# A two-layer graph network on one core: the end of each round put in another order

## The chip, the core and the metric

The kernel runs on one core of a Trainium2 chip. Such a core has five engines that work side by side: TensorE (PE) for matrix products and transposes, VectorE (DVE), ScalarE (ACT), GpSimd (POOL) and SyncE (SP). Each works through its own queue in the order in which the program was built. Here SP only issues transfers (DMAs). Matrix products land in PSUM, everything else lives in SBUF. The metric is the device time of one execution in microseconds (us), lower is better.

## The reference, cut to what matters

There are 64 graphs of 256 nodes with 512 features, each with its own 256 x 256 adjacency matrix. Two layers follow each other, both with a residual and a layer norm ahead of them.

```
h = relu(layernorm(x))                       # layer 0: gated attention, 8 heads of 64
q, k, v = h Wq', h Wk', h Wv'
attn = softmax(q k' / 8, masked by adj)      # per head
c = attn v
gate = sigmoid([c, h] Wg' + bg)
x = x + gate * h + (1 - gate) * c
h = relu(layernorm(x))                       # layer 1: one attention head with additive scores
Wh = h W
e = leaky_relu(Wh a1 + (Wh a2)'), masked by adj
x = x + elu(softmax(e) Wh)
```

All is float32.

## The kernel before

The kernel is a software pipeline over graphs. `emit_round(i)` (L480 to L544) writes one round, and the rounds run from -1 to 65. In a round, four graphs are in four stages: p = i + 1 gets its q, k, v and the first half of its scores, graph i gets its softmax and its weighted values c, q = i - 1 its gate, residual and Wh, and r = i - 2 its last attention and output. A graph's attention is done in two halves of four heads. Half 0 of the scores of graph p is computed at the end of the round before the one in which the rest of that graph's attention is done.

The steps of this case:

- `a_scores(g, half)` (L296): 16 matmul records on PE into four PSUM tiles of the pool "w", which has five buffers. It also takes the SBUF tile `e` for the exponentials.
- `a_softmax(g, half, jj)` (L314): for two heads, four passes on DVE that scale, mask and write `e` (L322), four exponentials on ACT (L326), a reciprocal on DVE (L330), and four multiplications on POOL (L333).
- `a_transpose(g, half)` (L337): four transposes of 32 x 32 blocks on DVE from `e` to `eb` (L344), and then 16 DMAs on SP from `eb` to `eT` (L349).
- `a_weigh(g, half)` (L352): 16 matmul records of v with `eT` (L362, tile `pc`), and a copy on ACT to `cT` (L135). In the second half it also forms the sums `S_c` on POOL (`token_sums`, L140 to L150): four operations, which the gate's products need.
- `g_gate`, `g_wh`, `p_qk`, `p_v`: products by Strassen's scheme (`strassen`, L152): seven block products in three parts, with three PSUM tiles ma, mb, mc that only these products use. Part 0 has products 1, 6 and 5, part 1 has 7 and 2, part 2 has 4 and 3. DVE and ACT combine them (L172, L176, L186). Product 6 of the gate is the first to read `S_c`, and it reads the second of the four sums (L147, `S_c<-S_c,cT`), which is made from the first one (L146).
- `g_diff` (L388): `d`, the difference of h and c, in two halves on POOL (L393).

Three things set the order. PE and SP run in the order in which `emit_round` writes them (`tc.manual_schedule`, L546). The order on DVE, ACT and POOL is chosen by the framework's scheduler when the program is built, so it can change where only the order of the calls changes. Buffers add waits of their own. The pool "e" has two buffers, and `e`, `eb` and `eT` all come from it in turn:

```
        "x": 5, "adj": 1, "mask": 4, "hT": 3, "S": 3, "qk": 3, "v": 2, "wh": 1, "e": 2,
```

So the tile `e` of the next graph's half 0 takes the buffer that held `eb` of the present graph's half 1. It cannot be written until the 16 DMAs that read that `eb` have landed. These are the DMAs that `a_weigh(i, 1)` waits for.

Of the kernel before, what the change touches and what calls it, by code (L numbers as in the profile page):

```python
# [22 lines left out]
def kernel(  # L23
# [78 lines left out]
    def weight_sums(key):  # L102

        w = weight[key]
        t = const.tile([P, 3, 2, w.shape[3]], F32, name=f"w{key}_t")
        b11, b12, b21, b22 = (w[:, r:r + 2, n, :] for r in (0, 2) for n in range(2))
        nc.vector.tensor_tensor(t[:, 1], b22, b12, ALU.subtract)
        nc.vector.tensor_tensor(t[:, 0], t[:, 1], b11, ALU.add)
        nc.vector.tensor_tensor(b12, b12, b11, ALU.subtract)
        nc.vector.tensor_tensor(t[:, 2], b21, t[:, 0], ALU.subtract)  # L110
        weight[key] = {1: b11, 2: b21, 3: b22, 4: t[:, 2], 5: b12, 6: t[:, 0], 7: t[:, 1]}
# [10 lines left out]
    def edge_columns():  # L122

        w = weight["1"]
        for c in range(HC):
            for side in range(2):
                scr = sb["tmp"].tile([P, 2, HH], F32, tag="t", name=f"scr_{c}_{side}")
                nc.vector.scalar_tensor_tensor(
                    scr, w[:, c, :, :HH], 1.0, a_sb[side].rearrange("p (n f) -> p n f", n=2),
                    ALU.mult, ALU.mult, accum_out=w[:, c, side, HH:],  # L130
                )
# [348 lines left out]
    def emit_round(i):  # L480


        parts = {}

        def step(fn, g, *args):
            if 0 <= g < B:
                fn(g, *args)

        def part(fn, g, n):
            if 0 <= g < B:  # L490
                if n == 0:
                    parts[fn] = fn(g)
                parts[fn][n]()

        p, q, r = i + 1, i - 1, i - 2
        step(load_graph, p + 1)
        part(g_gate, q, 0)
        step(a_softmax, i, 0, 1)
        step(g_diff, q)
        step(g_edges, r)  # L500
        part(g_gate, q, 1)
        step(p_sums, p)
        step(a_transpose, i, 0)
        part(g_gate, q, 2)
        step(g_mix, q)
        step(g_transpose, r)
        if i == -1:
            weight_sums("q")
            weight_sums("k")
        part(p_qk, p, 0)  # L510
        step(g_residual, q)
        step(g_out, r, 0)
        step(a_scores, i, 1)
        step(g_norm, q)
        step(a_softmax, i, 1, 0)
        part(p_qk, p, 1)
        step(a_weigh, i, 0)
        step(a_softmax, i, 1, 1)
        part(p_qk, p, 2)
        step(g_transpose_h, q)  # L520
        step(a_transpose, i, 1)
        if i == -1:
            weight_sums("v")
        part(p_v, p, 0)
        step(g_out, r, 1)
        if i == 0:
            weight_sums("gh")
            weight_sums("gc")
            nc.vector.tensor_scalar_mul(hbg, hbg, 0.5)
        part(p_v, p, 1)  # L530
        step(p_stats, p + 1)
        part(p_v, p, 2)
        if i == 0:
            edge_columns()
            weight_sums("1")
        part(g_wh, q, 0)
        step(p_norm, p + 1)
        step(p_transpose, p + 1)
        step(g_sums, i)
        step(a_weigh, i, 1)  # L540
        part(g_wh, q, 1)
        step(a_scores, p, 0)
        step(a_softmax, p, 0, 0)
        part(g_wh, q, 2)  # L544

    with tc.manual_schedule(engines={mybir.EngineType.PE, mybir.EngineType.SP}):  # L546
        load_graph(0)
        load_weight("q", nc.sync)
        load_weight("k", nc.scalar)
        load_weight("v", nc.sync)  # L550
        p_stats(0)
        p_norm(0)
        p_transpose(0)
        for i in range(-1, B + 2):
            if i == 0:
                load_weight("gh", nc.sync)
                load_weight("gc", nc.sync)
                load_weight("1", nc.sync)
                load_small()
            emit_round(i)  # L560
            graphs.pop(i - 2, None)
# [32 lines left out]
```

## Time and profile before

| | |
|---|---|
| three runs | 3481.12, 3485.15, 3485.97 us; median 3485.15 |
| profiled execution | span 3484.6 us, 68023 instructions, granted TensorE clock 0.991 |
| PE busy | 3324.3 us, 95% |
| DVE, POOL, ACT busy | 2294.7 us (66%), 1637.9 us (47%), 1338.4 us (38%) |
| DMA | 262.50 MB, mean 75 GB/s |

Busy time counts an engine's instructions alone. Matmuls are pipelined and their ends are modelled, so that the recorded end of one reaches a little past the start of the next. The waits of an engine are attributed to what came last, by semaphores. A round takes about 53 us. With PE at 95% what matters is what stands in the remaining time of PE: every wait of PE adds to the whole, while waits of the other engines cost nothing as long as PE has its next product in time.

### The profile page before, as it was taken

To read this page: it belongs to the slowest core of one execution; us is meant where nothing else is said; L and a number is where in the kernel's file an instruction comes from. 1 tells how busy PE (TensorE), PEld (TensorE's weight loads), DVE (VectorE), ACT (ScalarE), POOL (GpSimd) and SP (SyncE) were. 2 spreads that over 40 slices of the span, in tenths; PEclk is the share of its full clock that TensorE was granted. 3 is DMA by queue.
4 is the path that set the end of the run, shared out by engine and by line. 5 is a ranking of instruction groups with operands and counts; after the bars stand their busy time and mean duration, and the time that the engine had idled before them with its cause. 6 is when DMAs were issued, how large, how long until landed. Compare 5 with 4: busy or idle time off the path is not lost.

```text
span 3484.6 us, 68023 instructions
## 1 busy us (share of the span) xinstructions
PE 3324.3 (95%) x23944; PEld 2865.9 (82%) x23944; DVE 2294.7 (66%) x6184; ACT 1338.4 (38%) x3778; POOL 1637.9 (47%) x2439
## 2 busy tenths in 40 slices
PE   6999999999999999999999999999999999999996
PEld 5888888888888888888888888888888888888874
DVE  6666667667667667667666666676676676666653
ACT  2334334343344334334334343443433443333432
POOL 2454454454454454544544544544544545435433
PEclk9999999999999999999999999999999999999998
DMA  4232332322322322322323323323323223223221
GB/s 138 66 85 68 77 80 66 83 71 73 87 69 71 89 68 70 90 68 72 87 70 72 84 66 80 79 66 84 73 70 87 69 70 90 68 70 82 64 59 31
DMA packets 432195, 262.50 MB, mean 75 GB/s; under 512 B 310768, under 2 KB 333296, under 8 KB 431856
## 3 DMA queue, kind: packets, MB, share of 16 engines
q1 hardware_dynamic: 430800, 257.11, 30.0%
q8 instruction: 191, 3.13, 0.4%
q14 instruction: 148, 1.21, 0.1%
q10 hardware_dynamic: 1056, 1.05, 0.1%
HBM read 57.15 MB, written 33.55 MB: 26 GB/s over the span
## 4 chain that ended last, share of the span: by engine, by line
PE 59%; SPq 16%; DVE 12%; POOL 4%; DMA 4%; issue 3%; ACT 1%; DVEq 0%; POOLq 0%; ACTq 0%
SPq L349 16%; PE pmb_z L162 10%; PE pma_z L162 6%; PE pmc_z L162 6%; PE pmb_qk L162 6%; PE pc L362 5%; PE ps L306 5%; PE pma_qk L162 5%; PE pmc_qk L162 4%; PE pmb_wh L162 4%; DMA eT<-eb 4%; DVE e L322 2%; POOL e L333 2%; DVE bs_l L201 2%; PE pma_wh L162 2%
## 5 line engine op out<-in xcount | busy, mean ns | idle before, releaser
L333 POOL TENSOR_SCALAR e<-e,rec 128x256 f32<-128x256 f32 x1024 | 473.7, 482 | 256.0 <-DVE rec L330 133.5
L206 POOL TENSOR_TENSOR rs_l<-ve_l,mhalf 128x2 f32<-128x2 f32 x128 | 90.6, 708 | 1021.2 <-DVE ve_l L204 1017.3
L326 ACT ACTIVATE e<-e,low 128x256 f32<-128x256 f32 x1024 | 506.1, 496 | 84.3 <-DVE low L322 59.0
L322 DVE CUSTOM_DVE_ANT_0 e<-ps,mask 128x256 f32<-128x256 f32 x1024 | 375.1, 418 | 74.9 <-PE ps L306 71.6
L344 DVE STREAM_TRANSPOSE eb<-e 128x512 f32<-128x512 f32 x512 | 345.6, 694 | 88.4 <-POOL e L333 88.3
L362 PE MATMUL pc<-eT,v 128*64 128x256 f32 x2048 | 259.0, 396 | 111.7 <-DMA eT<-eb 103.0
L172 DVE TENSOR_TENSOR u_wh<-pmb_wh,u_wh 128x257 f32<-128x257 f32 x128 | 54.7, 427 | 408.7 <-PE pmb_wh L162 408.7
L472 ACT ACTIVATE pos<-po,rec 128x512 f32<-128x512 f32 x128 | 88.0, 687 | 604.6 <-DVE mv_l L202 415.3
L362 PEld LDWEIGHTS pc<-eT,v 128*64 128x64 f32 x2048 | 150.9, 140 | 193.4 <-issue 115.2
L306 PEld LDWEIGHTS ps<-qk 64*128 64x128 f32 x2048 | 187.3, 186 | 86.0 <-issue 68.8
L306 PE MATMUL ps<-qk 64*128 64x256 f32 x2048 | 255.7, 389 | 0.0
L465 PE MATMUL po<-wh,egT 128*128 128x512 f32 x512 | 245.8, 603 | 0.8 <-DVE egT L137 0.8
L444 ACT ACTIVATE eg<-eg,nm 128x256 f32<-128x256 f32 x128 | 64.0, 501 | 384.1 <-DVE nm L441 384.1
L475 POOL TENSOR_TENSOR x<-x,pos 128x512 f32<-128x512 f32 x128 | 163.0, 1274 | 98.0 <-DVE pos L474 98.0
L215 ACT ACTIVATE h_l<-x,nb_l,rs_l 128x512 f32<-128x512 f32 x256 | 201.8, 813 | 14.5 <-DVE nb_l L212 7.3
L135 ACT COPY cT<-pc 128x512 f32<-128x512 f32 x128 | 73.8, 577 | 327.6 <-PE pc L362 327.6
L326 ACT ACTIVATION_READ_ACCUMULATOR e<-e,low 128x1 f32 x1024 | 192.3, 188 | 0.0
L402 ACT ACTIVATE z<-z,hbg 128x256 f32<-128x256 f32 x256 | 116.2, 501 | 186.6 <-DVE z L172 186.6
L148 POOL TENSOR_TENSOR S_l<-hT_l 128x256 f32<-128x256 f32 x128 | 93.7, 732 | 166.5 <-DVE hT_l L137 166.5
L201 DVE BATCH_NORM_STATS2 bs_l<-x 128x6 f32<-128x512 f32 x256 | 167.8, 677 | 5.0 <-DMA x<-in_x_dram 5.0
L146 POOL TENSOR_TENSOR S_c<-cT 128x256 f32<-128x256 f32 x64 | 46.4, 725 | 255.2 <-ACT cT L135 255.2
L393 POOL TENSOR_TENSOR d<-hT_l,cT 128x512 f32<-128x512 f32 x128 | 162.5, 1270 | 0.0
(142 smaller groups left out, 8359.1 us busy)
## 6 DMA issues: line engine op xcount, KB each, us to landing
eT<-eb SPq DMA_DIRECT2D x2048, 64.0 KB, 2.0
x<-in_x_dram SPq DMA_DIRECT2D x64, 512.0 KB, 4.1
out_dram<-x SPq DMA_DIRECT2D x64, 512.0 KB, 2.9
hT_l<-h_l SPq DMA_DIRECT2D x1008, 32.0 KB, 2.0
adj<-in_adj_dram SPq DMA_DIRECT2D x64, 256.0 KB, 4.2
wk_sb<-in_L_gnn_Wk_dram ACTq DMA_DIRECT2D x2, 512.0 KB, 6.9
wq_sb<-in_L_gnn_Wq_dram SPq DMA_DIRECT2D x2, 512.0 KB, 8.7
wv_sb<-in_L_gnn_Wv_dram SPq DMA_DIRECT2D x2, 512.0 KB, 10.4
```

What stands on the lines that cost most here:

```text
L162: nc.tensor.matmul(bank[key][(slice(None), *cols)], lhsT, rhs, start=first and i == 0, stop=last and i == len(todo) - 1, skip_group_check= ...
L201: nc.vector.bn_stats(bs, xt[:, t, :])
L215: nc.scalar.activation(h[:, t, :], xt[:, t, :], AF.Relu, bias=nb[:, t:t + 1], scale=rs[:, t:t + 1])
L306: nc.tensor.matmul(psc[jj, i][:, t, :], qk[r:r + DK, 0, jj, t * P:(t + 1) * P], qk[r:r + DK, 1, jj, :], start=True, stop=True,)
L322: nc.vector.tensor_tensor_reduce(es[:, i, t, :], psc[jj, i][:, t, :], mask[:, t, :], -SCALE, HUGE, ALU.add, ALU.min, accum_out=low[:, i, t ...
L326: nc.scalar.activation(es[:, i, t, :], es[:, i, t, :], AF.Exp, bias=low[:, i, t:t + 1], scale=-1.0, accum_out=sums[:, i, t:t + 1],)
L333: nc.gpsimd.tensor_scalar(es[:, i, t, :], es[:, i, t, :], rec[:, i, t:t + 1], 1.0, ALU.mult, ALU.mult)
L344: nc.vector.transpose(blocks[:, :, 4 * h:4 * h + 4, :].rearrange("p b n c -> p n b c"), e[:, h])
L349: nc.sync.dma_start(eT[32 * j:32 * j + 32, i], blocks[32 * i:32 * i + 32, j])
L362: nc.tensor.matmul(pc[i * DK:(i + 1) * DK, jj, :].rearrange("p (t a c) -> p t a c", t=NT, c=32), s["v"][:, kc, hd * DK:(hd + 1) * DK], eT[ ...
L465: nc.tensor.matmul(pm, s["egT"][:, kc, t * P:(t + 1) * P], s["wh"][:, kc, :, :HH], start=(kc == 0), stop=(kc == NT - 1))
L475: nc.gpsimd.tensor_tensor(s["x"][:, t, :], s["x"][:, t, :], pos, ALU.add)
```

## The change

The calls at the end of the round are put in another order. Before, after part 0 of Wh, PE had: the weighted values of half 1 of graph i, Wh part 1, the scores of half 0 of graph p, Wh part 2. After it: the scores, Wh part 1, the weighted values, Wh part 2. The softmax that follows the scores (first two heads, `a_softmax(p, 0, 0)`) moves with them.

```
@@ -537,10 +537,10 @@
         step(p_norm, p + 1)
         step(p_transpose, p + 1)
         step(g_sums, i)
-        step(a_weigh, i, 1)
-        part(g_wh, q, 1)
         step(a_scores, p, 0)
         step(a_softmax, p, 0, 0)
+        part(g_wh, q, 1)
+        step(a_weigh, i, 1)
         part(g_wh, q, 2)
 
     with tc.manual_schedule(engines={mybir.EngineType.PE, mybir.EngineType.SP}):
```

The program holds the same instructions as before, in the same number on each engine. On PE two blocks change places. On SP nothing moves: none of the three steps issues a DMA. On POOL, as the program is built, a round of the middle now runs: one sum of `S_c` that needs only the first half of `cT` (L148), the four multiplications of the first two heads (L333), the four of the other two heads, then the first sum (L146), the second half of `d` (L393), the second sum (L147) and the fourth (L149). Before, these three sums and `d` stood ahead of the eight multiplications. On ACT the eight exponentials now stand ahead of the copy to `cT`, with the copy of Wh's product 2 (L186) between the seventh and the eighth. On DVE the eight passes now stand ahead of the additions of Wh part 1, but for the last pass, which follows the first of these additions.

More of the change, by code (lines that the diff above doesn't have):

```diff
@@ L539, in emit_round @@
         step(g_sums, i)
-        step(a_weigh, i, 1)
-        part(g_wh, q, 1)
         step(a_scores, p, 0)
         step(a_softmax, p, 0, 0)
+        part(g_wh, q, 1)
+        step(a_weigh, i, 1)
         part(g_wh, q, 2)
```

## The prediction

> **What bounds the kernel now.** I read the busy shares and the chain that ended last first.
>
> ```profile
> PE 3324.3 (95%) x23944; PEld 2865.9 (82%) x23944; DVE 2294.7 (66%) x6184; ACT 1338.4 (38%) x3778; POOL 1637.9 (47%) x2439
> PE 59%; SPq 16%; DVE 12%; POOL 4%; DMA 4%; issue 3%; ACT 1%; DVEq 0%; POOLq 0%; ACTq 0%
> ```
>
> PE is nearly full, yet 16% of the chain is SP's issuing: PE is overtaken by transfers somewhere. The second view was the waits of PE alone, from 130 to 3380 us, the 62 middle rounds (waited for; us, times, longest):
>
> ```profile
> PE pc L362 <- DMA eT<-eb: 86.5, 60, 2.6
> PE pc L362 <- issue: 3.7, 2, 2.1
> ```
>
> This is the whole answer: PE waits once a round, always ahead of `pc`, for 90.2 / 62 = 1.45 us on average. The timeline of PE over all rounds puts each of them at half 1; half 0 never waits. From one `pc` to the next a round takes 51.43 to 51.49 us plus its wait in nearly every round, so this wait decides the pace. The end of a round (start, us, instruction, idle before):
>
> ```profile
> 1719.99 1.03 PE L162 MATMUL pmc_wh<-w_sb,S_l 128*128 128x257 f32 x4
> 1722.11 1.95 PE L362 MATMUL pc<-eT,v 128*64 128x256 f32 x16 [1.09 <-DMA eT<-eb]
> 1723.98 1.14 PE L162 MATMUL pmb_wh<-w_t,S_l 128*128 128x257 f32 x4
> 1724.96 1.03 PE L162 MATMUL pma_wh<-w_sb,hT_l 128*128 128x257 f32 x4
> 1725.92 2.00 PE L306 MATMUL ps<-qk 64*128 64x256 f32 x16
> 1727.85 1.14 PE L162 MATMUL pmb_wh<-w_t,hT_l 128*128 128x257 f32 x4
> 1728.82 1.03 PE L162 MATMUL pmc_wh<-w_sb,S_l 128*128 128x257 f32 x4
> 1729.69 1.05 PE L162 MATMUL pma_z<-hT_l,wgh_sb 128*128 128x128 f32 x8
> 1730.58 1.06 PE L162 MATMUL pma_z<-cT,wgc_sb 128*128 128x128 f32 x8
> 1731.47 1.06 PE L162 MATMUL pmb_z<-S_g,wgh_t 128*128 128x128 f32 x8
> 1732.36 1.06 PE L162 MATMUL pmb_z<-S_c,wgc_t 128*128 128x128 f32 x8
> ```
>
> The reader is to see start-to-start spacings (ends overlap) and that `S_c` is needed last. The chain in time shows what releases `pc`: the last of 16 issues, each about 0.63 us, and its landing.
>
> ```profile
> 1720.00 1.98 DMA eT<-eb
> 1721.97 0.14 issue
> 1722.11 1.95 PE pc L362 x16
> ```
>
> Last, DVE and POOL in the same stretch:
>
> ```profile
> 1727.08 0.42 DVE L322 CUSTOM_DVE_ANT_0 e<-ps,mask 128x256 f32<-128x256 f32 x1 [1.03 <-PE ps L306]
> ...
> 1724.76 0.73 POOL L146 TENSOR_TENSOR S_c<-cT 128x256 f32<-128x256 f32 x1 [3.25 <-ACT cT L135]
> 1725.44 1.27 POOL L393 TENSOR_TENSOR d<-hT_l,cT 128x512 f32<-128x512 f32 x1
> 1726.67 0.73 POOL L147 TENSOR_TENSOR S_c<-S_c,cT 128x256 f32<-128x256 f32 x1
> ...
> 1729.93 1.85 POOL L333 TENSOR_SCALAR e<-e,rec 128x256 f32<-128x256 f32 x4 [1.73 <-DVE rec L330]
> 1732.10 1.85 POOL L333 TENSOR_SCALAR e<-e,rec 128x256 f32<-128x256 f32 x4 [0.32 <-DVE rec L330]
> ```
>
> Here the sums `S_c` are ready at 1727.4 and PE asks for them at 1732.36: 5 us to spare. The change spends this reserve.
>
> **What the Trainium skill says.** "Perfetto Trace Analysis", Per-instruction lifecycle: DVE, ACT and GpSimd run strictly first in, first out, and TensorE's ends are estimates. The trace agrees: `pmc_wh` ends at 1721.02 by the record while its successor, unhindered, would start at about 1720.95. "SBUF — State Buffer", The DMA setup-cost knee: every transfer pays about 2 us whatever its size, mostly for completion; here 1.98 us from issue to landing. "TensorE: Matmul & The Clock Gate", Part 1: the clock falls after an idle window of about 3.4 us. Here four records of `pmb_wh` take 1.93 us after a wait of 5.00 us near the end, and `pc` takes 1.95 us after 1.09 us as it does unhindered; waits of 1 us cost only themselves. The same page, Who interferes with whom: a DVE instruction with two SBUF inputs shuts out a GpSimd one that reads SBUF. The trace has it: the sum at L149 takes 1.17 us at 1717.19 beside such an instruction (L474), 0.73 us otherwise.
>
> **The change part by part.** Call T the moment at which PE takes up the scores. In the round shown T = 1719.99 + 0.96 = 1720.95 (0.96 is the step from `pma_wh` to `ps`).
>
> *Removed: the wait ahead of `pc`.* The scores (1.93) and Wh part 1 (0.97 and 0.96) come first, so PE reaches `pc` at T + 3.86. The transfers land at about T + w - 0.07, w being the recorded wait of before, at most 2.6 us in these rounds. It is hidden everywhere. With the 0.07 by which the record understates it, that is 1.52 us a round.
>
> *Not changed.* No instruction is added, SP's order is the same, and its next jobs (`out`, `hT`, the loads) stand as before. The chain to `eT` starts at the scores of half 1, with the same PE work up to T, so w keeps its size. The PSUM ring of five shifts by one: the scores take buffers whose holders (`pc` of half 0, the transposes) were copied out by 1712.3, `pc` takes that of `po`, read until 1716.5. Free.
>
> *Added: a wait on DVE.* The first pass of the softmax (L322) writes the buffer that `eb` of half 1 held, so it waits for the same 16 transfers. Before they had always landed. Call its start X. For want of a record I bound it: it can't start earlier than PE did with the same release (landing + 0.14, so T + w + 0.07), nor before T + 1.16 (as in the trace, 1725.92 to 1727.08); from above I allow 0.3 us more. I take 0.1 more, so X = T + w + 0.17, on average T + 1.62. Behind it on DVE stand seven passes, and the addition of Wh that frees bank b for product 4: it comes at X + 2.67, ends near T + 4.7, and product 4 follows at T + 5.74. Free.
>
> *Moved: `S_c` behind eight multiplications on POOL.* From X, by the distances of the trace: the exponentials start at X + 0.47 and follow each other every 0.49; the seventh at X + 3.43. Then ACT has the copy of Wh (0.25 a slot, as the copy `u_v` takes), so the eighth starts at X + 4.18 and its sum is out 0.59 later. The reciprocal follows 0.04 later, POOL 0.26 after that: the second four multiplications start at X + 5.07 (before: 1732.10 - 1727.08 = 5.02). The four take 1.81 from start to successor, the first sum 0.68, `d` 1.23, the second sum 0.73: done at X + 9.52. PE starts 0.06 after such an end (3409.52 to 3409.58). So `S_c` is there for PE at X + 9.58. The copy to `cT` is no limit: ACT is free at X + 4.8, `pc` done at T + 5.74, `cT` by T + 6.9, wanted at T + 8.48.
>
> *When PE wants it.* From T: scores 1.93, Wh 0.97 and 0.96, `pc` 1.88, Wh part 2 0.98 and 0.87, the gate's `hT`, `cT` and `S_g` blocks 0.89, 0.89 and 0.90. Sum T + 10.27.
>
> So a new wait of 1.62 + 9.58 - 10.27 = 0.93 us ahead of `pmb_z<-S_c` takes the place of 1.52: 0.59 us a round remains, 62 x 0.59 = 37 us. For the last graph, where no scores follow, Wh part 1 shortens the wait of 8.15 us by about 1.9. At the start I count nothing: a wait of 5.05 shrinks, but `S_c` comes later there too. In all 39 us from 3484.6, or 3445.6; the median of the three runs lies 0.55 above this profile: 3446.
>
> **The rivals.**
>
> *A, as worked out: 3446.* Its own range is 3430 to 3466: with X at its lower bound 43 + 2 us are gained, with 0.3 more only 25 + 2; the rest is for sizes on ACT and POOL.
>
> *B, the whole wait vanishes: 62 x 1.52 = 94, with the last graph 96, so 3389.* It needs `S_c` in time, 0.9 us earlier than worked out. For it speaks that POOL was 5 us early before; against it that eight multiplications of 0.46 and `d` stand ahead of it by the built order.
>
> *C, slower: POOL loses the shared port.* Place: the stretch from X + 5 to X + 9.5, where multiplications and sums run beside DVE. Price: 1.17 - 0.73 = 0.44 us for each collision. It decides from 0.59 us a round: two collisions make 0.88, a loss of 0.29 a round, 18 us, 3503. Against it: in that stretch DVE has block transposes with one input and additions with one input in PSUM, and POOL's multiplications kept 1.85 us beside such transposes (1730.90 and 1731.93).
>
> *D, it cancels: 3478 to 3492.* The same wait, only larger by 0.5 to 0.7 us, because DVE takes up its pass later than PE would have.
>
> **How the numbers follow.** A 0.70, B 0.10, D 0.08, C 0.12. Within 0.2% (7 us) is about what a measurement of this kernel can't tell from no change: faster 0.80, same 0.08, slower 0.12. The range from 3388 to 3482 takes in A, B and the spaces between, and leaves out C and half of D.
>
> **What would show it.** The waits of PE: none ahead of `pc`; one ahead of `pmb_z<-S_c`, released by POOL, 0.6 to 1.2 us in each round. DVE: its first pass waits for DMA `eT` in most rounds, and starts 1.2 to 1.7 us after the scores. POOL: multiplications, then the sums, without a gap. The span between rounds falls from about 52.9 to 52.3 us. The prediction is wrong if PE doesn't wait for `S_c` (B), if the second sum ends later than T + 11.8 (C, D), or if the wait ahead of `pc` stays.

## The result, and the profile after

The changed kernel takes 3445.75 us (median of 4 runs, 3444.50 to 3447.07). The kernel before, run beside it, takes 3483.99 us (median of 4 runs, 3481.12 to 3485.97). The ratio is 0.9891 [0.9874, 0.9908], so the reordering saves about 38 us. The profiled execution spans 3445.1 us against 3484.6 before.

The two lines of the page that were shown of before, now of after: busy times, then the shares of the chain that ended last.

```profile
PE 3333.9 (97%) x23944; PEld 2858.0 (83%) x23944; DVE 2280.1 (66%) x6184; ACT 1327.1 (39%) x3778; POOL 1639.2 (48%) x2439
PE 43%; SPq 15%; DVE 14%; POOL 13%; ACT 8%; DMA 4%; issue 3%; DVEq 0%; POOLq 0%; ACTq 0%
```

Each engine executes as many instructions as before. On the chain POOL rises from 4% to 13% and ACT from 1% to 8%, while PE falls from 59% to 43%. SP's issuing hardly moves (16% to 15%), so the transfers have not left the path. They now reach PE by another way.

The waits of PE after, from 130 to 3340 us (waited for; us, times, longest):

```profile
PE pmb_z L162 <- POOL S_c L147: 41.9, 61, 1.6
PE pc L362 <- DMA eT<-eb: 0.6, 1, 0.6
PE pmb_z L162 <- DVE u_z L172: 0.5, 1, 0.5
```

The wait ahead of `pc` is gone (one of 0.6 us is left). A new one stands in 61 rounds ahead of the first gate product that reads `S_c`, released by POOL. The end of a round on PE after (start, us, instruction, idle before):

```profile
1755.67 2.00 PE L306 MATMUL ps<-qk 64*128 64x256 f32 x16
1757.59 1.14 PE L162 MATMUL pmb_wh<-w_t,S_l 128*128 128x257 f32 x4
1758.57 1.03 PE L162 MATMUL pma_wh<-w_sb,hT_l 128*128 128x257 f32 x4
1759.53 1.95 PE L362 MATMUL pc<-eT,v 128*64 128x256 f32 x16
...
1765.03 1.06 PE L162 MATMUL pmb_z<-S_g,wgh_t 128*128 128x128 f32 x8
1766.61 1.16 PE L162 MATMUL pmb_z<-S_c,wgc_t 128*128 128x128 f32 x8 [0.53 <-POOL S_c L147]
1767.61 1.06 PE L162 MATMUL pmc_z<-S_g,wgh_sb 128*128 128x128 f32 x8
```

`pc` starts 3.86 us after the scores, without a wait. What releases `S_c` is read from the chain in time, in the same round (some short pieces are left out):

```profile
1754.72 1.99 DMA eT<-eb
1756.71 0.04 DVEq L322
...
1757.03 0.43 DVE e L322
1757.49 3.55 ACT e L326 x14
1761.04 0.26 ACT wh L186
1761.30 0.24 ACT e L326
1761.83 0.19 DVE rec L330
1762.11 1.85 POOL e L333 x4
1763.95 0.69 POOL S_c L146
1764.65 1.23 POOL d L393
1765.88 0.69 POOL S_c L147
1766.61 1.16 PE pmb_z L162 x8
```

This is one unbroken path. The last transfer lands at 1756.71, DVE takes up the first pass of the softmax at 1757.03, ACT works through the exponentials (with the copy of Wh among them), POOL multiplies and sums, and PE starts at the end of the second sum. The transfer that used to release `pc` now releases this path, which has 9.58 us to run before PE may go on.

### The profile page after: what moved, and what is told of

Read it like the earlier page. It is cut to its first block, busy times and chain, and to the rows that moved or that the text cites. A ratio compares the mean times of both kernels' runs of the same rounds, so it can differ in the third digit from the quotient of the medians.

```text
span 3445.1 us, 68154 instructions
## 1 busy us (share of the span) xinstructions
PE 3333.9 (97%) x23944; PEld 2858.0 (83%) x23944; DVE 2280.1 (66%) x6184; ACT 1327.1 (39%) x3778; POOL 1639.2 (48%) x2439
## 4 chain that ended last, share of the span: by engine, by line
PE 43%; SPq 15%; DVE 14%; POOL 13%; ACT 8%; DMA 4%; issue 3%; DVEq 0%; POOLq 0%; ACTq 0%
SPq L349 14%; PE pmb_z L162 9%; ACT e L326 7%; PE pmc_z L162 6%; POOL e L333 6%; PE pmb_qk L162 6%; PE pma_qk L162 4%; PE pmc_qk L162 4%; DVE e L322 4%; PE pma_z L162 3%; DMA eT<-eb 3%; DVE bs_l L201 2%; POOL d L393 2%; PE po L465 2%; POOL rs_l L206 2%
## 5 line engine op out<-in xcount | busy, mean ns | idle before, releaser
L333 POOL TENSOR_SCALAR e<-e,rec 128x256 f32<-128x256 f32 x1024 | 473.7, 482 | 406.2 <-DVE rec L330 183.6
L344 DVE STREAM_TRANSPOSE eb<-e 128x512 f32<-128x512 f32 x512 | 337.6, 686 | 31.5 <-POOL e L333 31.3
L362 PEld LDWEIGHTS pc<-eT,v 128*64 128x64 f32 x2048 | 138.3, 138 | 106.0 <-issue 40.4
L162 PE MATMUL pmb_z<-S_c,wgc_t 128*128 128x128 f32 x1024 | 141.6, 281 | 42.7 <-POOL S_c L147 42.7
L148 POOL TENSOR_TENSOR S_l<-hT_l 128x256 f32<-128x256 f32 x128 | 95.1, 743 | 164.8 <-DVE hT_l L137 164.8
L162 PEld LDWEIGHTS pmb_z<-S_c,wgc_t 128*128 128x128 f32 x1024 | 124.3, 191 | 54.5 <-POOL S_c L147 54.5
L172 DVE TENSOR_TENSOR u_z<-pmb_z,u_z 128x256 f32<-128x256 f32 x128 | 53.6, 419 | 173.5 <-issue 168.2
L393 POOL TENSOR_TENSOR d<-hT_l,cT 128x512 f32<-128x512 f32 x128 | 162.7, 1271 | 0.0
```

Source lines behind the costliest of these rows:

```text
L162: nc.tensor.matmul(bank[key][(slice(None), *cols)], lhsT, rhs, start=first and i == 0, stop=last and i == len(todo) - 1, skip_group_check= ...
L333: nc.gpsimd.tensor_scalar(es[:, i, t, :], es[:, i, t, :], rec[:, i, t:t + 1], 1.0, ALU.mult, ALU.mult)
L344: nc.vector.transpose(blocks[:, :, 4 * h:4 * h + 4, :].rearrange("p b n c -> p n b c"), e[:, h])
L362: nc.tensor.matmul(pc[i * DK:(i + 1) * DK, jj, :].rearrange("p (t a c) -> p t a c", t=NT, c=32), s["v"][:, kc, hd * DK:(hd + 1) * DK], eT[ ...
L393: nc.gpsimd.tensor_tensor(d, s["hT"][:, :, js, :], s["cT"][:, :, js, :], ALU.subtract)
```

## The experiments

In kernels with added lines, line numbers lie 1 to 4 higher than in the code above. The kernel before stood at 3484 to 3490 us in these sessions; ratios are against its runs beside them. Diffs are cut to the lines that matter, and are against the changed kernel unless the text says otherwise. Theory 1 is the prediction's: the first pass waits for the transfers, and `S_c` comes late behind the multiplications and `d`. Theory 2 is the rival that `S_c` is late because `cT` is, whatever stands ahead of it on POOL.

**Leave out the second four multiplications.**

```diff
         nc.vector.reciprocal(rec, sums)
+        if half == 0 and jj:
+            return
         for i in range(2):
```

> The changed kernel without the second four of the eight multiplications on POOL (heads three and four of half 0 stay unnormalised, so this part of the computation is left out). Theory 1, the queue on POOL: the sums S_c no longer stand behind these four, the first sum starts when cT is there (about 6.8 us after the scores), the second is done at 9.5, PE wants it at 10.3: the wait ahead of the gate's S_c block goes to nearly nothing, 0.8 us x 62 = 50 us less, about 3395 us (3388 to 3405). Theory 2, the late cT: the sums are late because the weighted values themselves come 3.9 us later, whatever POOL does before: the wait stays at 0.6 to 0.7 us by the record, about 3446 us.

Measured: 3387.15 us (3383.11 to 3388.94), ratio 0.971 [0.9695, 0.9724], just under the range expected of theory 1. POOL and PE in a round whose scores start at 1728.41:

```profile
1735.20 0.73 POOL L146 TENSOR_TENSOR S_c<-cT 128x256 f32<-128x256 f32 x1 [0.64 <-ACT cT L135]
1737.11 0.73 POOL L147 TENSOR_TENSOR S_c<-S_c,cT 128x256 f32<-128x256 f32 x1
1738.66 1.06 PE L162 MATMUL pmb_z<-S_c,wgc_t 128*128 128x128 f32 x8
```

`cT` now releases the first sum, 6.8 us after the scores, and still the second sum is done 0.8 us before PE wants it. `cT` itself is as late as in the changed kernel: its copy ends 6.7 us after the scores, there 6.6. Theory 2 falls: `cT` as late as that does not make PE wait once these four multiplications are gone.

**Move `d` behind the sums, leaving nothing out.**

```diff
         step(a_softmax, i, 0, 1)
-        step(g_diff, q)
         step(g_edges, r)
         part(g_gate, q, 1)
+        step(g_diff, q)
         step(p_sums, p)
```

> The changed kernel with the difference d asked for after part 1 of the gate, so that on POOL both halves of d stand behind the sums and not between the first and the second. Theory 1: the second sum comes 1.23 us earlier, a wait is left only where the softmax's first pass starts more than 1.9 us after the scores, about 0.1 us on average: 45 us less, about 3400 us. Theory 2 (late cT): the sums then end 8.2 us after the scores, also in time: 3400 as well. A third theory, that POOL is not what PE waits for but what the semaphores name last: no change, 3446 us. If d comes too late for the gate's mix, DVE and then py would wait: more than 3400.

Measured: 3392.62 us (3390.87 to 3392.99), ratio 0.9726 [0.971, 0.9742]. POOL:

```profile
1736.13 1.85 POOL L333 TENSOR_SCALAR e<-e,rec 128x256 f32<-128x256 f32 x4 [0.39 <-DVE rec L330]
1737.94 0.74 POOL L146 TENSOR_TENSOR S_c<-cT 128x256 f32<-128x256 f32 x1
1738.76 0.73 POOL L147 TENSOR_TENSOR S_c<-S_c,cT 128x256 f32<-128x256 f32 x1
```

Without `d` between the sums, the second ends 8.43 us after the first pass of the softmax instead of 9.54. The wait at `S_c` falls from 41.9 to 1.7 us in the middle rounds, and the round to 51.40 us. This run doesn't part theories 1 and 2, which expect the same of it, but it shows that PE does wait for POOL. One call moved by a few lines is worth more than the change itself.

**The same move in the kernel before.** The edit is that of the experiment before, made in the kernel before.

> The kernel before with the difference d asked for after part 1 of the gate, as in the faster variant of the changed kernel. In the kernel before the sums S_c are ready 5 us ahead of PE, so 1.2 us more are worth nothing. Theory 1: no change, 3485 us (within 0.2% of the kernel before). A theory by which the late d itself is what made that variant fast: about 50 us less, 3435 us.

Measured: 3489.76 us, ratio 1.0015 [1.0008, 1.0022]. It gains nothing, and loses 0.15%. Of the 5.8 us between the two profiled runs, 2.8 are longer waits of PE and 1.3 are slower `pc` after such waits, both in the middle rounds; no run tested this. `d` became costly only when the change had spent the reserve of `S_c`.

**Wh part 1 ahead of the weighted values, the scores after them.** Against the kernel before, only these two change places; the diff is against the changed kernel.

```diff
         step(g_sums, i)
-        step(a_scores, p, 0)
-        step(a_softmax, p, 0, 0)
         part(g_wh, q, 1)
         step(a_weigh, i, 1)
+        step(a_scores, p, 0)
+        step(a_softmax, p, 0, 0)
         part(g_wh, q, 2)
```

> The end of the round in the order Wh part 1, weighted values, scores with their softmax, Wh part 2: against the kernel before only Wh part 1 and the weighted values change places. pc has 1.93 us of PE work in front of it, the transfers are up to 2.5 us late but 1.45 on average; from the scores on everything follows as in the kernel before, so the softmax's pass meets no busy buffer, and the addition that the gate's product 7 needs stands as early on DVE as before. Theory 1: a few rounds keep a wait of up to 0.6 us ahead of pc, about 3 us in all; nothing else: 3391 us (3386 to 3397). Rival, that any place between Wh and the gate costs a wait of its own (as Wh parts 1 and 2 ahead of the values did): above 3400 us.

Measured: 3381.26 us (3379.39 to 3382.06), ratio 0.9703 [0.969, 0.9716]: the best of all, and it beats both kernels. It is 10 us less than expected, below the range. PE:

```profile
1724.09 1.03 PE L162 MATMUL pmb_wh<-w_t,S_l 128*128 128x257 f32 x4
1724.96 1.03 PE L162 MATMUL pma_wh<-w_sb,hT_l 128*128 128x257 f32 x4
1725.91 1.95 PE L362 MATMUL pc<-eT,v 128*64 128x256 f32 x16
1727.79 2.00 PE L306 MATMUL ps<-qk 64*128 64x256 f32 x16
1729.72 1.14 PE L162 MATMUL pmb_wh<-w_t,hT_l 128*128 128x257 f32 x4
```

Part 1 alone (here 1.82 us, 1724.09 to 1725.91) covers the average wait of 1.52: in the middle rounds 3.6 us of waiting in all are left ahead of `pc`, and the gate's product runs without a wait. The round takes 51.26 us, less than the 51.4 that were taken for a round without waits; the last section says why. The scores between the parts were thus more cover than the wait needed, and their early start did nothing for the softmax, which waits for the transfers.

**Both parts of Wh first.**

```diff
         step(g_sums, i)
-        step(a_scores, p, 0)
-        step(a_softmax, p, 0, 0)
         part(g_wh, q, 1)
-        step(a_weigh, i, 1)
         part(g_wh, q, 2)
+        step(a_weigh, i, 1)
+        step(a_scores, p, 0)
+        step(a_softmax, p, 0, 0)
```

> Another order at the end of the round: Wh part 1, Wh part 2, the weighted values, then the scores and their softmax. The transfers have 3.8 us of PE work in front of pc, as in the changed kernel, but the sums S_c stand ahead of the eight multiplications on POOL, and the softmax's pass comes after pc, so its buffer is long free. Theory 1: no wait of PE is left in the middle rounds; 51.4 us a round instead of 52.3, about 3389 us (3383 to 3397). Theory 2 (late cT): the sums have the scores (1.9) and 2.7 us of the gate to be ready, enough, 3389 as well. A theory by which the gain came from having the scores early: 3446 to 3485.

Measured: 3461.87 us (3460.32 to 3463.22), ratio 0.9926 [0.9911, 0.994]: a miss by 73 us. The waits ahead of `pc` and `S_c` are gone in the middle rounds, but there is a third one (waits of PE there, then DVE and PE in one round):

```profile
PE pmb_z L162 <- DVE u_z L172: 75.0, 61, 1.2
```

```profile
1779.70 0.71 DVE L344 STREAM_TRANSPOSE eb<-e 128x512 f32<-128x512 f32 x1 [1.06 <-POOL e L333]
1780.34 0.39 DVE L172 TENSOR_TENSOR u_z<-pmb_z,u_z 128x256 f32<-128x256 f32 x1
1780.78 1.16 PE L162 MATMUL pmb_z<-S_g,wgh_t 128*128 128x128 f32 x8 [1.23 <-DVE u_z L172]
```

The addition that frees a PSUM tile of the gate stands on DVE behind a transpose, and that transpose waits for POOL's multiplications. The time lies where the expectation put a gain from early scores, but the trace shows this wait instead, and the order of the experiment before is the fastest without early scores. A softmax that starts too late cost more here (75.0 us of waiting) than one that delays `S_c` (41.9).

**Three buffers in the pool "e", to take the transfers' release away from the softmax.** To make room, "tmp" has 3 buffers instead of 6, and five small tiles 2 instead of 4. A control has that smaller room with "e" at 2.

```diff
-        "x": 5, "adj": 1, "mask": 4, "hT": 3, "S": 3, "qk": 3, "v": 2, "wh": 1, "e": 2,
-        "cT": 1, "z": 1, "h": 1, "tmp": 6, "U": 3,
+        "x": 5, "adj": 1, "mask": 4, "hT": 3, "S": 3, "qk": 3, "v": 2, "wh": 1, "e": 3,
+        "cT": 1, "z": 1, "h": 1, "tmp": 3, "U": 3,
```

> The changed kernel with three buffers instead of two for e, eb and eT, so that the softmax's first pass finds a buffer that no transfer reads (room is made with three buffers instead of six for the pool tmp and two instead of four for five small tiles). The order on POOL is the same. Theory 1: the first pass starts 1.16 us after the scores in every round instead of 1.56 on average, and the whole chain to the second sum with it; the wait ahead of the gate's S_c block falls by 0.4 us to about 0.35 by the record, and is nearly the same in every round: 62 x 0.4 = 25 us less than the changed kernel, 3421 us (3415 to 3428). Rival: the buffer plays no part, the pass starts late for PE's or DVE's own reasons: 3446 us.

> Control to the kernel with three buffers: the changed kernel with the same smaller pools (tmp three, five small tiles two), and two buffers for e, eb and eT as in the changed kernel. All theories: the smaller pools add no wait that PE sees, 3446 us (3443 to 3450). If it is slower, the three-buffer kernel has to be compared with this one.

The control: 3448.05 us, ratio 0.9896 [0.9882, 0.9909], as the changed kernel, with its wait. Three buffers: 3471.90 us (3470.47 to 3473.28), ratio 0.9963 [0.9951, 0.9976], slower than the control. Waits of PE in the middle rounds with three buffers:

```profile
PE pmb_v L163 <- DVE qk L173: 44.9, 60, 0.8
PE pmb_z L163 <- POOL S_c L148: 17.3, 61, 0.3
```

The softmax starts 1.16 us after the scores in every round, the lower bound of the prediction, and the wait at `S_c` falls to 0.3 us. In most rounds this proves nothing about the buffer: PE's new wait comes ahead of the scores, and the transfers have mostly landed about 0.1 us before these start, so they would have held no softmax with two buffers either. But in five rounds they land 1.27 to 2.96 us after the start of the scores, and the softmax still starts at 1.16, ahead of the landing, which it does in no round of this order with two buffers. There the mechanism shows. In one of them, whose scores start at 81.48, SP is still issuing the sixteen transfers when DVE starts:

```profile
72.72 10.25 SPq L350 DMA_DIRECT2D eT<-eb  x16
82.64 0.43 DVE L323 CUSTOM_DVE_ANT_0 e<-ps,mask 128x256 f32<-128x256 f32 x1 [0.63 <-PE ps L307]
```

The time is missed, because the builder also put the additions of `qk` later on DVE, and PE waits for these at `pmb_v`. So the worth of removing only the buffer's wait was not measured.

**Two spare transfers ahead of the sixteen.**

```diff
+    spare = const.tile([32, 2, P], F32, name="spare")
...
+        if half:
+            for n in range(2):
+                nc.sync.dma_start(spare[:, n], blocks[:32, 0, 4 * n:4 * n + 4, :].rearrange("p n c -> p (n c)"))
         for i in range(4):
```

> The changed kernel with two spare DMAs of 16 KB each from eb to an unused tile ahead of the 16 of half 1, so that these land about 1.2 us later (two issues of about 0.6 us). Theory 1 (the softmax's first pass waits for the same transfers through its buffer): pc still has its reserve of 3.9 us and doesn't wait, but the first pass, the multiplications and the sums all come 1.2 us later: the wait ahead of the gate's S_c block grows from 0.8 to about 2.0 us, 3446 + 75 = 3520 us (3500 to 3530). Theory 2 (late cT) or any in which the buffer plays no part: pc's reserve hides it, 3446 us (up to 3450).

Measured: 3447.67 us, ratio 0.9885 [0.9871, 0.99]: it tested nothing. SP's queue:

```profile
1744.47 1.14 SPq L350 DMA_DIRECT2D spare<-eb  x2
1746.62 10.01 SPq L353 DMA_DIRECT2D eT<-eb  x16
```

The spare transfers read blocks that are ready early, so SP issued them in time that it would have spent waiting: a gap of 1.0 us lies between. Two further kernels read the last blocks instead (`12 + 2 * n:14 + 2 * n`), one in the changed order and one in the order of before (with a smaller spare tile).

> The changed kernel, with two spare transfers from the eb of half 1, issued on SP ahead of its sixteen. Unlike those of e3_two_dmas they read the blocks of the last transpose, so SP can issue them only when eb is complete, and the sixteen come two issues later, 2 x 0.63 = 1.27 us. Theory 1 (the landing releases the softmax's first pass, and the wait ahead of the gate's product follows it one for one): the first pass starts 1.2 to 1.3 us later, the wait ahead of pmb_z<-S_c grows from 0.8 to about 2.1 us, the time is 3446 + 62 x 1.27 = 3525 (3510 to 3535). Theory 2 (the wait is set by something that the landing does not move, such as the multiplications' queue on POOL or the late cT): no change, 3446 to 3455.

> The kernel before, with the same two spare transfers. The wait ahead of pc should grow by 1.27 us a round under either theory: 3485 + 62 x 1.27 = 3564 (3550 to 3575), and the difference between the two orders should stay at about 39 us under theory 1, while under theory 2 it grows to about 110.

In the changed order: 3521.62 us, ratio 1.0091 [1.0074, 1.0108], in the range of theory 1, but not by its path. The first pass starts 3.88 us after the scores instead of 1.57: 2.3 us later where 1.2 to 1.3 were expected, because the softmax of half 1, which the transfers wait for, also ends about 0.9 us later. The pass still follows the landing, by 0.12 to 0.76 us. Yet PE starts at `S_c` only 0.14 us later than without the spare transfers. POOL shows why:

```profile
1751.39 0.74 POOL L147 TENSOR_TENSOR S_c<-cT 128x256 f32<-128x256 f32 x1
1752.08 1.27 POOL L397 TENSOR_TENSOR d<-hT_l,cT 128x512 f32<-128x512 f32 x1
1753.31 0.73 POOL L148 TENSOR_TENSOR S_c<-S_c,cT 128x256 f32<-128x256 f32 x1
1754.12 0.73 POOL L150 TENSOR_TENSOR S_c<-cT,S_c 128x256 f32<-128x256 f32 x1
1754.82 1.39 POOL L334 TENSOR_SCALAR e<-e,rec 128x256 f32<-128x256 f32 x3
```

The built order changed, and the sums now stand ahead of the second four multiplications. So PE starts at `S_c` 7.35 to 7.42 us after the first pass instead of 9.6, which makes up for the later landing. What is late then is the wait of the experiment with both parts of Wh first (`u_z`, 31.3 us in all). So a later landing makes this order slower, but this run does not show a wait at `S_c` that grows with it.

In the order of before: 3617.26 us (3615.73 to 3625.70), ratio 1.0374 [1.0359, 1.039], where 3564 was expected. The wait at `pc` grew about as expected, from 1.45 to 2.82 us a round on average. Two rounds of PE, one slow and one not, show where the rest is:

```profile
580.81 3.44 PE L366 MATMUL pc<-eT,v 128*64 128x256 f32 x16 [2.57 <-DMA eT<-eb]
...
1732.10 1.95 PE L366 MATMUL pc<-eT,v 128*64 128x256 f32 x16 [2.69 <-DMA eT<-eb]
```

After waits of 2.57 us or more, 26 of 61 `pc` take longer than 2.05 us, mostly 3.3 to 3.7 instead of 1.95 (37 us in all), and in some rounds Wh part 1 is slow too. The granted clock is 0.54 from 580.8 to 584.2 us, and 1.00 from 1732.0 to 1735.5. Its mean in this trace is 0.977, in that of the kernel before 0.991.

The two orders thus differ by 96 us with the spare transfers, nearer to the 110 of theory 2 than to the 39 of theory 1. That decides nothing: in one kernel the queue ahead of `S_c` became shorter, in the other the clock was lost, and neither sum had taken this in.

## Why the prediction held, step by step

- **The wait removed.** Right: `pc` starts at T + 3.86, unhindered, in all but one of the middle rounds. A little was missed: in before, `pc` ran slowly after four waits of 2.14 to 2.64 us (3.53 us after 2.53, for one), 4.7 us in all, which vanish too.
- **The wait on DVE.** Right in kind, and sized well: X lies 1.57 us after T on average where 1.62 was taken, and later than the bound of 1.16 in all 62 rounds. (The profile puts most of these waits down to PE's scores, but the pass starts after the landing in every round, and in before, where the transfers had landed, it starts at T + 1.16.) Two errors partly cancel. The delay from landing to start was short: 0.24 was taken, from one round of PE (0.14) and 0.1 more, while DVE needs 0.29 us on average (0.12 to 0.77). The landing was taken too late: PE's own delay is 0.22 on average over the rounds of before (0.04 to 0.46), not 0.14, so the transfers landed there at T + 1.30, not T + 1.38; after, they land at T + 1.28.
- **`S_c` behind the multiplications.** X + 9.58 was worked out, and PE starts at X + 9.58 to 9.60 in nearly every round. The second four multiplications start at X + 5.08 (5.07) and the second sum ends at X + 9.54 (9.52). Durations from the trace of before and the queue order of the changed program as built were enough.
- **When PE wants it.** T + 10.27; PE gets it at T + 11.10 on average. The wait is 0.83 us, where 0.93 was worked out. But it costs 0.11 more than itself: the product after it starts 1.00 us later (1766.61 to 1767.61), not 0.89 as on average in before. The term was thus 0.10 too large, and this price was missing.
- **The sum.** Between the same transposes of an early and a late round the rounds lose 52.91 - 52.27 = 0.64 us each (0.59 foreseen): 1.52 - 0.83 - 0.11 = 0.58, and the slow `pc` of before, 4.7 / 62 = 0.08, less 0.02 for two small waits that are left. That makes 39.5 us of 62 rounds where 37 were foreseen.
- **The last graph.** Wrong in effect, right in the wait: the wait ahead of `pc` falls from 8.15 to 6.00 us, 2.15 where 1.9 was said. But `pc` starts when its transfers land, so the gain has to come after it, where two products fewer stand. It does at first: from `pc` to the transposes `py` after 21.06 us, before 22.52. Then `po` takes 3.04 us where it took 1.89, and from `pc` to the end of the trace after needs 63.5 us, before 63.3. Nothing is left of the 1.9. The granted clock is 0.50 from 3404.7 to 3408.1 us, where `po` runs; before it is 1.00 in the like stretch (3444.0 to 3450.5). Why it was lower there was not tested. So the total of 39 us (39.5 between the profiled runs) is met more closely than its parts: the middle rounds gained 2.5 us more than foreseen, the last graph 2 us less, and that they cancel is luck.
- **Held at nothing.** The PSUM ring, the addition of Wh and the copy to `cT`: no wait for any of these in the middle rounds, but one of 0.5 us for an addition of the gate.
- **The rivals.** B (all of the wait vanishes, 3389) is what happens as soon as `d` leaves the queue: 3392.62. The prediction's remark that B needs `S_c` 0.9 us earlier is confirmed by that run, which brought it 1.1 us earlier. C, collisions on the shared port, did not happen: four multiplications take 1.85 us and each sum 0.73, as before. (The rule on two SBUF inputs behind C stands in the Trainium skill's "SBUF — State Buffer", Who interferes with whom; the prediction's "the same page" reads as if it were the page on TensorE.) D took DVE's delay as larger than PE's; it is, by 0.07 us on average, less than the 0.5 that D needed.

Not settled: what the wait on DVE costs alone, since each way of removing it changed the built order elsewhere too.

## What to carry to other kernels

Moving a consumer behind other work hides its wait, but a transfer that also frees a buffer still releases somebody: follow the buffer to its next writer, and that writer's queue down to the bound engine. Move only as much ahead of the wait as covers it: here 1.82 us of products for 1.52 us of waiting gave 3381 us, while the larger move, which put eight multiplications and `d` ahead of a sum, gave 3446. Where a framework orders the other engines, read the built order of every variant before trusting a sum made for another one: here it turned one experiment into a loss and gave another its expected time by another path.

## What the runs showed of the hardware that was not expected

- A wait costs PE more than its length where no change of shape follows it: the first group of products after it takes 1.00 us to its successor instead of 0.89.
- A change between products of 128 rows and 64-row or 64-column ones costs about 0.1 us (0.96 to 0.98 from start to start instead of 0.87). With `pc` and `ps` side by side there are fewer such changes, and the round is 51.26 us against 51.40 in the kernel with `d` moved, though neither waits.
- Waits of PE of about 2 us and more can go with a loss of its clock. Each slow `pc` of the middle rounds overlaps a stretch of 3.41 us, or twice that, in which the granted clock is 0.50. With the spare transfers in the order of before, 26 of 61 waits of 2.57 us or more were followed by one, while two of 3.33 us were not. In the kernel before it had happened after 2.14 us, and with `d` moved in it after 1.96. "TensorE: Matmul & The Clock Gate", Part 1, of the Trainium skill names an idle window of about 3.4 us; the runs here show the loss after shorter waits, not always, and so waits of 2 to 3.4 us have an uncertain price.
